# Gathers that skip the lanes without an edge, and a tile's first two slots added up later

## The chip, the cores and the metric

The kernel runs on one core of a Trainium2 chip. The metric is the device time of one execution in microseconds, the median of several runs. The core's engines each work through a queue of their own in order and wait for each other by semaphores: TensorE (PE in the profile; PEld are its weight loads), VectorE (DVE), ScalarE (ACT), GpSimd (POOL) and SyncE (SP). DMAs are issued by SyncE, ScalarE and GpSimd and run on 16 DMA engines. A gather, in which every partition fetches a row that an index in its memory names, is issued by GpSimd.

## What is computed

Two graph layers on 4096 nodes with 512 features. `adj` is a 4096 x 4096 matrix with about 8 nonzero weights a row beside the diagonal.

```python
# layer 0
a = adj + eye
d = sum(a, axis=1) ** -0.5
out = relu((d[:, None] * a * d[None, :]) @ x @ W.T + b)
x = layernorm(x + out)
# layer 1: attention whose scores are -1e16 wherever adj < 1 (off the diagonal too)
x = layernorm(x + attention(x, adj, Wks, Wqs, Wvs, Wo))
```

As the weights lie below 1, each row of layer 1 attends to itself alone, and the layer is a product with a fixed matrix. The kernel tests on the chip that this holds and has a general version behind a branch, which does not run with these inputs.

## The kernel before

The 4096 rows are 32 tiles of 128 rows. `few_edges_below_one` does the work in two halves.

**First half.** In a loop over tiles (L1064) the rows of `adj` are streamed in. ScalarE sums each row (`sum_rows`, L708) or the negative part of it (`sum_negative`), GpSimd makes the scaling d from it (`scaling`), and y = d * (x @ W.T) is computed tile by tile and stored to HBM (`keep_y`). SyncE loads the adjacency tiles: 13 of them pass through two buffers (`a_n`, pool `passing`), which ScalarE's sum frees; the others (`a_t`) have five. Along the way the weights of layer 1 are folded into one matrix `wvo` (`second_weights`): a generator hands out one step per turn of the loop, whose second part is run in the next turn (`left`, L1090). Its last step, `centre` (L650), subtracts column means on VectorE, which also gives row sums, and then shifts `wvo` by the row means in four activations on ScalarE.

**Finding the edges.** VectorE scans each tile of `adj` in eight segments of 512 columns. `MAX8` (L752) gives the eight largest values of a segment and `FIND_INDEX8` (L753) their columns. `sorting` packs segment, column and value bits into integer keys (`place` holds the segment's and the place's code), takes the 24 largest keys and unpacks from them column and weight. A key of 0 stands for no edge. `match` then hands the edges that a row has beyond nine to other lanes of the same tile that have room, by a permutation in a matmul, so that each tile ends with KH = 9 slots of 128 lanes: an index (`cols_all`), a weight and a target row each (`wr_all`). `match_end` (L890) writes them. A lane without an edge gets column 0 and weight 0. Scans, sorting and matching of the later tiles go on through most of the second half, spread over its steps (`some`).

**Second half.** The loop over tiles and slots (L1306, L1313) has 32 x 9 steps. In each step:

- `gather` (L1119, issued at L1124) makes GpSimd fetch the 128 rows of y for a slot that is AHEAD = 18 steps ahead, into one of 19 buffers `g`. A gather waits for its buffer's last reader.
- `build` makes ScalarE write the 128 x 128 matrix `s_t` for a slot (`spread`), which carries weights to target rows.
- TensorE multiplies it with the gathered rows and adds into the tile's sum `zs` in PSUM (L1337). In the trace each such product is two matmuls.
- `presum` (L1137): in tiles 1 to 22 the first two slots of a tile stay in their own rows. So they are added up beforehand: ScalarE scales slot 0 (L1141) at step 7 of the tile before, VectorE multiplies slot 1 by its weight and adds it (L1143) at step 8, and one product serves both, at step 0 of the tile. In the last nine tiles five slots are treated so.
- After a tile's last product, `scaled` and `residual` (VectorE), transposes and the product with `wvo` (TensorE, L703), variance and `finish` (ScalarE) make its output one to three tiles later.

The instructions are written in this order; the framework's scheduler sets the final order on each engine and the buffers, except where an instruction is marked to stay in place.

Of the kernel before, what the change touches and what calls it, by code (L numbers as in the profile page):

```python
# [11 lines left out]
ALU = mybir.AluOpType  # L12
# [407 lines left out]
def few_edges_below_one(  # L420
# [18 lines left out]
    nc = tc.nc  # L439
# [74 lines left out]
            ranks(sources[:, n + 1, lane + 1 - width : lane + 1], -2, 2 * r - 1 - P)  # L514

    place = const.tile([P, 2, C], U32, name="place")
    for f, (per_seg, per_edge, base, shift) in enumerate(
        ((-(C - 1), -SEGS, C * SEGS, 21), (-E, -1, C, 24))
    ):
        nc.gpsimd.iota(  # L520
            place[:, f], pattern=[[per_seg, SEGS], [per_edge, E]], base=base, channel_multiplier=0
        )
        nc.vector.tensor_scalar(place[:, f], place[:, f], shift, None, op0=ALU.logical_shift_left)


    v_all = const.tile([P, NT, C], FP, name="v_all")
# [31 lines left out]
    resident = list(range(last, NT))  # L558
    again = [t for t in range(last) if t not in early]
    order = early + resident + again  # L560
    def load_first(t, parts=1):
        if t in early or t in resident:
            return load_a(t, parts=2 if t == NT - 1 else parts)
        return load_a(t, pn, "a_n")
# [52 lines left out]
    def second_weights(su1):  # L617

        wo_sb, wvT = su1[:, 0], su1[:, 1]

        def transposed(r):
            pt = ps_t.tile([P, 512], FP, name="pt")
            for j in range(ND):
                nc.tensor.transpose(pt[:, ts(j, P)], w_nat[:, j, ts(r, P)], ident)
            return pt

        def put(r, pt):
            nc.scalar.copy(
                wvT[:, r, :].rearrange("q (p j) -> q j p", j=ND),
                pt[:, :D].rearrange("q (j p) -> q j p", j=ND),  # L630
            )

        def product(dc):
            pa = ps_a.tile([P, D], FP, name="acc")
            for r in range(NP):
                nc.tensor.matmul(
                    pa, wvT[:, r, ts(dc, P)], wo_sb[:, r, :], start=(r == 0), stop=(r == NP - 1)
                )
            return pa

        def add(dc, pa):
            nc.scalar.copy(wvo[:, dc, :], pa)
            nc.gpsimd.tensor_tensor(wvo[:, dc, ts(dc, P)], wvo[:, dc, ts(dc, P)], ident, ALU.add)

        def sums():
            pa = ps_a.tile([P, D], FP, name="acc")
            for dc in range(ND):
                nc.tensor.matmul(pa, ones, wvo[:, dc, :], start=(dc == 0), stop=(dc == ND - 1))
            return pa

        def centre(pa):
            row = const.tile([P, ND], FP, name="row")
            for dc in range(ND):
                nc.vector.scalar_tensor_tensor(
                    wvo[:, dc, :], pa, -1.0 / D, wvo[:, dc, :], op0=ALU.mult, op1=ALU.add,
                    accum_out=row[:, dc : dc + 1],
                )
            nc.vector.tensor_scalar(row, row, -1.0 / D, None, op0=ALU.mult)
            for dc in range(ND):
                nc.scalar.activation(  # L660
                    wvo[:, dc, :], wvo[:, dc, :], AF.Identity, bias=row[:, dc : dc + 1]
                )

        for r in range(NP):
            yield "t", (lambda r=r: transposed(r)), (lambda pt, r=r: put(r, pt))
        for dc in range(ND):
            yield "p", (lambda dc=dc: product(dc)), (lambda pa, dc=dc: add(dc, pa))
        yield "p", sums, centre

    def load_keys():  # L670
        su2 = setup_tile()
# [84 lines left out]
    def sorting(t, idx, rec):  # L756
# [16 lines left out]
        def stt(out, a, sc, b, op0, op1, **kw):  # L773
            return lambda: nc.vector.scalar_tensor_tensor(out, a, sc, b, op0=op0, op1=op1, **kw)  # L774
# [10 lines left out]
        def drop(f, r):  # L785
# [5 lines left out]

                stt(own, idx[:, home], spot[:, t % TS : t % TS + 1], v[:, home],
                    ALU.is_equal, ALU.mult, accum_out=own_all[:, t : t + 1]),
                stt(key[:, 0], idx, 12, place[:, 0], ALU.logical_shift_left, ALU.bitwise_or),
            ],
            [
                stt(key[:, 1], vu, 0x7FFFF, place[:, 1], ALU.bitwise_and, ALU.bitwise_or),
# [18 lines left out]
            [  # L816
                one(ints[:, 1], topu[:, 0], 0xFFF, 19, op0=ALU.bitwise_and,
                    op1=ALU.logical_shift_left),
                one(ints[:, 0], topu[:, 0], 12, 0xFFF, op0=ALU.logical_shift_right,
                    op1=ALU.bitwise_and),  # L820
            ],
            [
# [67 lines left out]
    def match_end(t, merged):  # L890
        wr = wr_all[:, t]
        nc.vector.tensor_copy(wr[:, 0:3], merged[:, 0:3])
        nc.vector.tensor_tensor(wr[:, 0:3], wr[:, 0:3], merged[:, 3:6], ALU.add)
        nc.vector.tensor_tensor(wr[:, 1], wr[:, 1], merged[:, 6], ALU.add)
        nc.vector.tensor_scalar(cols_all[:, t], wr[:, 0], float(N - 1), None, op0=ALU.min)
        if second:
            nc.scalar.activation(wr[:, 3], wr[:, 1], AF.Copy, scale=-1.0)
        else:
            nc.vector.tensor_scalar(wr[:, 3], wr[:, 1], -1.0, None, op0=ALU.mult)
# [160 lines left out]
        a_tiles[t] = load_first(t)  # L1060
    transpose_w()
    split_b()
    setup, left = iter(()), None
    for t in range(NT + 1):  # L1064
        if t == 0:
            su1 = load_second_weights()
        if t + DEEP < NT:
            a_tiles[t + DEEP] = load_first(t + DEEP)
        if t == 3:
            order_second_weights()  # L1070
            setup = second_weights(su1)

        ahead = sum(at <= projected(t) for at, _ in due)
        turn = sum(at <= projected(t + (t >= LEAD)) for at, _ in due)
        turn_rows(turn, 3)
        kind, begin, end = next(setup, (None,) * 3) if ahead - done[1] < 2 else (None,) * 3
        got = begin() if kind == "t" else None
        if t < NT:
            if t in early:
                sum_negative(t, a_tiles[t])  # L1080
            else:
                sum_rows(deg_all[:, t : t + 1], a_tiles[t][:, : N // 2 if t == NT - 1 else N])
                more = None
                if t == NT - 1:
                    more = small.tile([P, 1], FP, name="more")
                    sum_rows(more, a_tiles[t][:, N // 2 :])
                scaling(t, more)
            if t in again:
                del a_tiles[t]
        if left:  # L1090
            left()
            left = None
        for j in [j for at, j in due if at == t]:
            keep_y(j, us.pop(j))
        while done[1] < ahead:
            j = due[done[1]][1]
            us[j] = times(evacuate(p1, "xT", turned.pop(j), t >= NT - 7), wT)
            done[1] += 1
        turn_rows(turn, 2)
        if kind == "t":  # L1100
            end(got)
        if kind == "p":
            left = lambda end=end, pa=begin(): end(pa)
        if t < NT - 5:
            match(*ALL)
        some((t + 1) * RATE)
# [4 lines left out]

    mat = ctx.enter_context(tc.tile_pool(name="mats", bufs=3))
    p2 = ctx.enter_context(tc.tile_pool(name="second", bufs=2))
    AHEAD = 18

    summed = [1] + [2] * (NT - 1 - 9) + [SAME] * 9
    slots = {}

    def gather(j):  # L1119
        if j >= NT * KH:  # L1120
            return
        t, k = order[j // KH], j % KH
        slots[j] = p2.tile([P, D], FP, name="g", bufs=AHEAD + 1)
        nc.gpsimd.indirect_dma_start(  # L1124
            out=slots[j], out_offset=None, in_=y[:, :],
            in_offset=bass.IndirectOffsetOnAxis(ap=cols_all[:, t, k : k + 1], axis=0),
        )

    def load_own(i):
# [7 lines left out]
    def presum(i, k):  # L1137
        g = slots[i * KH]
        w = wr_all[:, order[i], 1, k : k + 1]
        if k == 0:  # L1140
            nc.scalar.activation(g, g, AF.Copy, scale=w)  # L1141
            return
        nc.vector.scalar_tensor_tensor(  # L1143
            g, slots.pop(i * KH + k), w, g, op0=ALU.mult, op1=ALU.add
        )

    def last_products(ks, c):

# [157 lines left out]
    for i in range(NT + 2):  # L1306
# [6 lines left out]
        for k in range(KH):  # L1313
# [7 lines left out]
            if i == NT - 1:  # L1321
# [8 lines left out]
                if k == 7:  # L1330
                    pts[i] = transpose_rows(hs[i], (0, 1))
                    hTs[i] = p2.tile([P, ND, P], FP, name="hT", bufs=2)
                    tc.keep_in_program_order(nc.scalar.copy(
                        hTs[i][:, 0:2].rearrange("p c s -> p (c s)"), pts[i][:, : 2 * P]
                    ))
            elif i < NT and not 0 < k < summed[i]:
                nc.tensor.matmul(  # L1337
                    zs[i], mats[i][:, KH if k < summed[i] > 1 else k, :], slots.pop(i * KH + k),
                    start=False, stop=(k == KH - 1),
                )  # L1340
            if i < NT:
                gather(i * KH + k + AHEAD)
            build(1)
            if i + 1 < NT and k >= KH - summed[i + 1] and summed[i + 1] > 1:
                presum(i + 1, k - (KH - summed[i + 1]))
            if k == 1 and has_p and not ends:
                scaled(p)
# [74 lines left out]
```

## Time and profile before

| | |
|---|---|
| median of 3 runs | 631.8 us (629.84 to 633.22) |
| profiled execution | 632.17 us, of it 630.3 us span |
| VectorE, TensorE, ScalarE, GpSimd busy | 555.0, 523.2, 497.7, 357.6 us |
| bytes moved | 217.68 MB, mean 345 GB/s |
| first gather begins, last ends | 220.8 us, 606.9 us |
| software queue (GpSimd's DMAs) | 28,192 packets, 92.30 MB |

The span is cut into 40 slices of 15.76 us in the page; a digit is the busy share of a slice in tenths.

```profile
PE   1599886699968052799897999999999999989793
DVE  5699999999999998799998999999999999854441
ACT  0859668688899858479978988998989899877751
POOL 5232323233323277677775667777777777777740
PEclk9999988999999566799998999999999999989898
DMA  8999999899999587999999999999999988888851
```

The first half ends in the fourteenth slice, where DMA and TensorE drop; from there on the gathers run. In a row of a group, the numbers behind the bar are the busy time in us and the mean of one in ns, and behind the next bar the idle time of the engine just before these instructions, with what ended most of it. In the timeline a row has its start, its duration, engine, line, operation and tiles, and in brackets the idle time before it and its releaser.

### The profile page before, as it was taken

The numbers are of one execution on the slowest core, as the hardware profiler recorded it, in microseconds if no ns is written. First come the engines' busy times: TensorE is split into PE (matmuls) and PEld (weight loads), VectorE is DVE, ScalarE is ACT, GpSimd is POOL, SyncE is SP. The second block draws the span as 40 slices with busy tenths as digits, with TensorE's granted clock in tenths as the row PEclk, the third lists the DMA queues.
The fourth block names the chain that finished last, engine by engine and source line by source line (L and its number), as shares of the span: only waits on it lengthen the run. The fifth ranks groups of instructions, "written<-read, shape, count | busy, mean of one in ns | idle before, by whom it ended". The sixth has DMA issues, their size and how long they took to land. (4 is left out here: it accounts for less than half of the span.)

```text
span 630.3 us, 7782 instructions
## 1 busy us (share of the span) xinstructions
PE 523.2 (83%) x1537; PEld 241.2 (38%) x1537; DVE 555.0 (88%) x2037; ACT 497.7 (79%) x1093; POOL 357.6 (57%) x465
## 2 busy tenths in 40 slices
PE   1599886699968052799897999999999999989793
PEld 1344333345423021344443444444444444433251
DVE  5699999999999998799998999999999999854441
ACT  0859668688899858479978988998989899877751
POOL 5232323233323277677775667777777777777740
PEclk9999988999999566799998999999999999989898
DMA  8999999899999587999999999999999988888851
GB/s 327 401 420 423 421 427 428 332 416 426 425 425 424 238 282 226 354 383 397 398 397 399 402 368 327 389 354 381 313 394 366 317 265 280 280 276 244 286 163 38
DMA packets 57273, 217.68 MB, mean 345 GB/s; under 512 B 8701, under 2 KB 9981, under 8 KB 52864
## 3 DMA queue, kind: packets, MB, share of 16 engines
q1 hardware_dynamic: 23888, 115.48, 46.1%
q0 software_dynamic: 28192, 92.30, 41.7%
q10 hardware_dynamic: 5136, 9.31, 4.0%
q14 instruction: 43, 0.35, 0.2%
q8 instruction: 14, 0.23, 0.1%
HBM read 200.28 MB, written 16.78 MB: 344 GB/s over the span
## 5 line engine op out<-in xcount | busy, mean ns | idle before, releaser
L1124 POOL DMA_INDIRECT g<-y,cols_all x288 | 286.9, 996 | 101.9 <-issue 46.6
L1337 PE MATMUL acc<-g,s_t 128*128 128x512 f32 x450 | 221.6, 626 | 38.4 <-DVE g L1143 22.2
L752 DVE MAX8 v_all<-a_t 128x8 f32<-128x512 f32 x256 | 166.7, 678 | 15.9 <-DMA a_t<-in_adj_dram 15.9
L753 DVE FIND_INDEX8 idx<-v_all,a_t 128x8 uint32<-128x512 f32 x256 | 173.2, 684 | 0.0
L703 PE MATMUL acc<-wT,xT 128*128 128x512 f32 x256 | 121.8, 625 | 20.6 <-ACT xT L694 19.8
L1337 PEld LDWEIGHTS acc<-g,s_t 128*128 128x128 f32 x450 | 84.2, 199 | 133.0 <-issue 101.0
L703 PE MATMUL acc<-wvo,hT 128*128 128x512 f32 x256 | 117.8, 602 | 5.2 <-ACT hT L694 4.2
L715 ACT ACTIVATE dump<-a_t 128x2048 uint8<-128x2048 f32 (+1 forms) x50 | 119.2, 2383 | 0.0
L703 PEld LDWEIGHTS acc<-wT,xT 128*128 128x128 f32 x256 | 49.2, 200 | 78.1 <-issue 53.1
L703 PEld LDWEIGHTS acc<-wvo,hT 128*128 128x128 f32 x256 | 48.8, 193 | 66.9 <-issue 57.0
L1006 ACT ACTIVATE sq<-cols,wr_all 128x128 f32<-128x128 f32 x160 | 58.8, 393 | 6.7 <-DMA a_t<-in_adj_dram 6.1
L1143 DVE SCALAR_TENSOR_TENSOR g<-g,wr_all 128x512 f32<-128x512 f32 x58 | 43.0, 741 | 23.4 <-ACT s_t L1016 6.6
L1010 ACT ACTIVATE s_t<-sq,wr_all 128x128 f32<-128x128 f32 x128 | 58.5, 485 | 0.2
L722 POOL TENSOR_SCALAR deg<-deg_all 128x1 f32<-128x1 f32 x32 | 7.3, 229 | 78.5 <-DVE deg_all L970 45.5
L710 ACT ACTIVATE dump<-a_n 128x4096 uint8<-128x4096 f32 x13 | 47.3, 3639 | 0.0
L550 POOL DMA_DIRECT2D x_t<-in_x_dram x32 | 18.0, 565 | 41.6 <-PE pt L689 35.4
L783 DVE MAX8 top<-key 128x8 f32<-128x64 f32 x192 | 36.2, 213 | 0.1
L1141 ACT ACTIVATE g<-g,wr_all 128x512 f32<-128x512 f32 x31 | 22.1, 713 | 16.4 <-issue 10.0
L694 ACT COPY hT<-pt 128x512 f32<-128x512 f32 x31 | 18.0, 579 | 18.1 <-PE pt L689 17.9
L774 DVE SCALAR_TENSOR_TENSOR key<-key,top 128x64 f32<-128x64 f32 x128 | 32.2, 272 | 0.0
L694 ACT COPY xT<-pt 128x512 f32<-128x512 f32 x32 | 18.9, 600 | 14.3 <-PE pt L689 12.4
L1194 DVE SCALAR_TENSOR_TENSOR h<-yo,own_all,acc 128x512 f32<-128x512 f32 (+1 forms) x33 | 23.7, 719 | 5.1 <-PE acc L1337 2.6
(135 smaller groups left out, 661.4 us busy)
## 6 DMA issues: line engine op xcount, KB each, us to landing
a_t<-in_adj_dram SPq DMA_DIRECT2D x17, 2048.0 KB, 21.5
a_t<-in_adj_dram SPq DMA_DIRECT2D x56, 512.0 KB, 12.4
a_n<-in_adj_dram SPq DMA_DIRECT2D x13, 2048.0 KB, 15.8
x_t<-in_x_dram POOLq DMA_DIRECT2D x32, 256.0 KB, 11.3
yo<-y SPq DMA_DIRECT2D x32, 256.0 KB, 6.5
x_t<-in_x_dram SPq DMA_DIRECT2D x32, 256.0 KB, 7.3
out_dram<-r_t ACTq DMA_DIRECT2D x31, 256.0 KB, 6.1
y<-y_t POOLq DMA_DIRECT2D x18, 256.0 KB, 14.7
```

The costliest lines, as they stand in the source:

```text
L694: copy = nc.scalar.copy(dst.rearrange("p c s -> p (c s)"), pt[:, :D])
L703: nc.tensor.matmul(u, srcT[:, dc, :], w[:, dc, :], start=(dc == 0), stop=(dc == ND - 1))
L710: nc.scalar.activation(dump[:, : part.shape[1]], part, AF.Copy, accum_out=dst)
L715: nc.scalar.activation(dump[:, o], a_t[:, o], AF.Relu, scale=-1.0, accum_out=neg_all[:, t, halves[0] : halves[0] + 1],)
L752: long.append(lambda o=o, seg=seg: nc.vector.max(v[:, o], seg))
L753: long.append(lambda o=o, seg=seg: nc.vector.max_index(idx[:, o], v[:, o], seg))
L783: return lambda: nc.vector.max(top[:, f, r * 8 : r * 8 + 8], keyf[:, f])
L1006: nc.scalar.activation(sq, cols1, AF.Square, bias=wr[:, 2, k : k + 1])
L1010: nc.scalar.activation(s_t[:, k, :], away(), AF.Relu, scale=wr[:, 3, k : k + 1], bias=wr[:, 1, k : k + 1],)
L1124: nc.gpsimd.indirect_dma_start(out=slots[j], out_offset=None, in_=y[:, :], in_offset=bass.IndirectOffsetOnAxis(ap=cols_all[:, t, k : k + 1 ...
L1143: nc.vector.scalar_tensor_tensor(g, slots.pop(i * KH + k), w, g, op0=ALU.mult, op1=ALU.add)
L1337: nc.tensor.matmul(zs[i], mats[i][:, KH if k < summed[i] > 1 else k, :], slots.pop(i * KH + k), start=False, stop=(k == KH - 1),)
```

## The change

**Indices.** The keys are built so that a lane without an edge comes out as index 8191 instead of 0, beyond the 4096 rows, and the real ones as 8191 minus a number of 4096 and more. `place` is made of other numbers, an `or` in the key becomes an `xor`, the mask of the index has 13 bits for 12, and `match_end` turns the number around in place of a minimum with N - 1. `gather` is given a bound, N - 1, and told that an index beyond it is no error: such a row is skipped, and its lane keeps what the buffer held. In the first three tiles, whose gathers fill the 19 buffers for the first time, an operation more forces a valid index (`unskipped`).

**First two slots.** In tiles 1 to 22 the scaling comes at step 8 of the tile before, the multiply-add at step 1 of the tile, their product at step BASE = 3. Slots 2, 3 and 4 are multiplied at steps 0, 1 and 2, slots 5 to 8 at steps 4 to 7, and step 8 has no product.

**Shift of `wvo`.** The four activations at the end of `centre` become a step of their own, `shift`, run a turn of the first half's loop later.

```diff
@@ few_edges_below_one: codes of the keys
-        ((-(C - 1), -SEGS, C * SEGS, 21), (-E, -1, C, 24))
-    ):
+    per_code = 2 * SEGS
+        (per_code * E - 1, per_code, per_code - 1, N.bit_length() - 1 + 12 - (SEGS.bit_length() - 1), (SW - 1) << 12),
+        (E, 1, 1, 24, 0),
+    )):
...
-        nc.vector.tensor_scalar(place[:, f], place[:, f], shift, None, op0=ALU.logical_shift_left)
+        nc.vector.tensor_scalar(
+            place[:, f], place[:, f], shift, fill,
+            op0=ALU.logical_shift_left, op1=ALU.bitwise_or,
+        )
@@
+    AHEAD = 18
+    ABSENT = 2 * N - 1
+    unskipped = order[: -(-(AHEAD + 1) // KH)]
@@ second_weights: centre
             nc.vector.tensor_scalar(row, row, -1.0 / D, None, op0=ALU.mult)
+            return row
+
+        def shift(row):
             for dc in range(ND):
-                nc.scalar.activation(
+                tc.keep_in_program_order(nc.scalar.activation(
                     wvo[:, dc, :], wvo[:, dc, :], AF.Identity, bias=row[:, dc : dc + 1]
-                )
+                ))
...
         yield "p", sums, centre
+        yield "s", None, shift
@@ sorting
-                stt(key[:, 0], idx, 12, place[:, 0], ALU.logical_shift_left, ALU.bitwise_or),
+                stt(key[:, 0], idx, 12, place[:, 0], ALU.logical_shift_left, ALU.bitwise_xor),
...
-                one(ints[:, 0], topu[:, 0], 12, 0xFFF, op0=ALU.logical_shift_right,
+                one(ints[:, 0], topu[:, 0], 12, ABSENT, op0=ALU.logical_shift_right,
@@ match_end
-        nc.vector.tensor_scalar(cols_all[:, t], wr[:, 0], float(N - 1), None, op0=ALU.min)
+        if t in unskipped:
+            nc.vector.tensor_scalar(
+                wr[:, 0], wr[:, 0], float(ABSENT - (N - 1)), None, op0=ALU.max
+            )
+        nc.vector.tensor_scalar(
+            cols_all[:, t], wr[:, 0], -1.0, float(ABSENT), op0=ALU.mult, op1=ALU.add
+        )
@@ loop of the first half
-        if left:
-            left()
-            left = None
+        row = (left() if left else None) or row
+        left = None
...
+        if kind == "s":
+            left = lambda end=end, row=row: end(row)
@@ gather
             in_offset=bass.IndirectOffsetOnAxis(ap=cols_all[:, t, k : k + 1], axis=0),
+            bounds_check=N - 1, oob_is_err=False,
@@ loop of the second half
+    BASE = 3
...
+    def product(i, m, j, stop):
+
+        nc.tensor.matmul(zs[i], mats[i][:, m, :], slots.pop(j), start=False, stop=stop)
...
+            elif i < NT and summed[i] == 2:
+                if k == BASE:
+                    product(i, KH, i * KH, False)
+                else:
+                    m = k + 2 if k < BASE else k + 1
+                    if m < KH:
+                        product(i, m, i * KH + m, m == KH - 1)
             elif i < NT and not 0 < k < summed[i]:
-                nc.tensor.matmul(
-                    zs[i], mats[i][:, KH if k < summed[i] > 1 else k, :], slots.pop(i * KH + k),
-                    start=False, stop=(k == KH - 1),
-                )
+                product(i, KH if k < summed[i] > 1 else k, i * KH + k, k == KH - 1)
...
-            if i + 1 < NT and k >= KH - summed[i + 1] and summed[i + 1] > 1:
+            if i + 1 < NT and summed[i + 1] == 2 and k == KH - 1:
+                presum(i + 1, 0)
+            if i < NT and summed[i] == 2 and k == 1:
+                presum(i, 1)
+            if i + 1 < NT and k >= KH - summed[i + 1] and summed[i + 1] > 2:
                 presum(i + 1, k - (KH - summed[i + 1]))
```

More of the change, by code (lines that the diff above doesn't have):

```diff
@@ L516, in few_edges_below_one @@
     place = const.tile([P, 2, C], U32, name="place")
-    for f, (per_seg, per_edge, base, shift) in enumerate(
-        ((-(C - 1), -SEGS, C * SEGS, 21), (-E, -1, C, 24))
-    ):
+    per_code = 2 * SEGS
+    for f, (per_seg, per_edge, base, shift, fill) in enumerate((
+        (per_code * E - 1, per_code, per_code - 1, N.bit_length() - 1 + 12 - (SEGS.bit_length() - 1), (SW - 1) << 12),
+        (E, 1, 1, 24, 0),
+    )):
         nc.gpsimd.iota(
@@ L1062, in few_edges_below_one @@
     split_b()
-    setup, left = iter(()), None
+    setup, left, row = iter(()), None, None
     for t in range(NT + 1):
@@ L1113, in few_edges_below_one @@
     p2 = ctx.enter_context(tc.tile_pool(name="second", bufs=2))
-    AHEAD = 18
+    BASE = 3
     summed = [1] + [2] * (NT - 1 - 9) + [SAME] * 9
```

## The prediction

> **What bounds the kernel.** I read the page first (busy shares, then the forty slices), then the groups, then GpSimd's own timeline and sums over stretches. The page's busy shares mislead here:
>
> ```profile
> PE 523.2 (83%) x1537; PEld 241.2 (38%) x1537; DVE 555.0 (88%) x2037; ACT 497.7 (79%) x1093; POOL 357.6 (57%) x465
> L1124 POOL DMA_INDIRECT g<-y,cols_all x288 | 286.9, 996 | 101.9 <-issue 46.6
> L550 POOL DMA_DIRECT2D x_t<-in_x_dram x32 | 18.0, 565 | 41.6 <-PE pt L689 35.4
> L722 POOL TENSOR_SCALAR deg<-deg_all 128x1 f32<-128x1 f32 x32 | 7.3, 229 | 78.5 <-DVE deg_all L970 45.5
> ```
>
> GpSimd looks like the idlest engine at 57%. But 286.9 us of it lie in one line, the 288 gathers of the second half, and 101.9 us of idle time sit directly before them, put down mostly to "issue", a wait for nothing that the profile shows. The timeline of GpSimd explains this:
>
> ```profile
> 333.83 0.94 POOL L1124 DMA_INDIRECT g<-y,cols_all  x1 [0.30 <-DMA g<-y,cols_all]
> 336.53 0.94 POOL L1124 DMA_INDIRECT g<-y,cols_all  x1 [1.75 <-PE acc L1337]
> 337.77 0.95 POOL L1124 DMA_INDIRECT g<-y,cols_all  x1 [0.30 <-DVE rec L780]
> 339.02 0.95 POOL L1124 DMA_INDIRECT g<-y,cols_all  x1 [0.30 <-issue]
> 342.51 1.09 POOL L1124 DMA_INDIRECT g<-y,cols_all  x1 [2.54 <-DVE key L774]
> ```
>
> Whatever is named as releaser, the smallest gap is 0.30 us. So a gather costs 0.95 + 0.30 = 1.25 us of GpSimd (206 of the 287 steps from one gather to the next are below 1.26 us). The first begins at 220.8 and the last ends at 606.9, 386.2 us, of which 288 x 1.25 = 360 us is this price, 14.5 us are gathers longer than 0.946 us (63 of them), and 11.9 us (summed over the timeline) are gaps beyond 0.30, like the 1.75 and 2.54 above. **The second half is a queue of gathers**; everything else fits beside it or just does not:
>
> ```profile
> 440.00:518.00 78.00, 78.00 (x236) 35.35 (x235) 77.95 (x322) 72.42 (x213) 59.28 (x60) 1.00 0.94 334
> ```
>
> In this stretch (its columns: length, PE, PEld, DVE, ACT, POOL busy, clock, DMA) 60 gathers x 0.30 + 59.28 = 77.3 of 78 us: GpSimd is full, and so is TensorE, which takes 11.54 us for a tile of nine gathers where GpSimd takes 11.25 us and some 0.4 of lengthening. Two engines are tied. TensorE falls behind only where it idles:
>
> ```profile
> 236.99 0.32 PE L855 MATMUL pt<-ident,rank_key 128*128 128x128 f32 x1
> 248.27 10.18 PE L1337 MATMUL acc<-g,s_t 128*128 128x512 f32 x16 [10.96 <-DVE g L1143]
> 263.13 1.22 PE L1337 MATMUL acc<-g,s_t 128*128 128x512 f32 x1 [4.14 <-DVE g L1143]
> ```
>
> These are the waits for the presum, the multiply-add of a tile's first two slots on VectorE: 22.2 us in 8 waits. Each leaves the ring of 19 buffers full later, and GpSimd then waits for "PE acc L1337": the 11.9 us.
>
> **The change, part by part.**
>
> *Presum later.* For tiles 1 to 22 the scaling moves one step, the multiply-add two steps, and their product three steps later; the products of slots 2, 3 and 4 come before it. Nothing is added: same instructions, same queues, 32 x 9 gathers. The product of a slot takes two matmuls, 2 x 0.43 = 0.86 us, so 2.6 us of work now stand ahead of the wait. From the 10.96 and the 4.14 us waits that takes 2.6 each; the waits of 1.62, 0.59, 0.94 and 1.29 us at 314, 327, 342 and 369 go whole (VectorE has 4 steps where it had 2). Sum 9.6 us. The two late waits (1.02 and 1.67 us, after 545) are of tiles with five summed slots, which don't change. What is late next is GpSimd, so this is not 9.6 us of its own: it is the larger part of the 11.9 us of GpSimd's excess gaps, and counts once. Slots 2 to 4 are needed two steps (2.5 us) earlier, 16 steps or 20 us after their issue; they land in 6.7 us (longest 11.2). Slot 0's buffer is held three steps longer, slot 2's to 8's less; when the buffers come free in order, the lead falls from 18 to 16 steps, at most 2 x 1.25 = 2.5 us once.
>
> *The shift of wvo, moved to the next turn of the first half.* ScalarE stood there for VectorE's row sums:
>
> ```profile
> 116.59 2.56 ACT L660 ACTIVATE wvo<-wvo,row 128x512 f32<-128x512 f32 x4 [4.01 <-DVE row L658]
> GB/s 327 401 420 423 421 427 428 332 416 426 425 425 424 238 282 226 354 383 397 398 397 399 402 368 327 389 354 381 313 394 366 317 265 280 280 276 244 286 163 38
> ```
>
> The eighth slice (110 to 126 us) moves 332 GB/s where its neighbours move 428 and 416: (422 - 332) x 15.76 us / 422 = 3.4 us of lost transfer in a stage that DMA fills to the end, since the next adjacency load waits for the buffer that the late row sum on ScalarE frees. The 4.01 us wait goes, the four activations stay. I take -3 us; ends 0 (other gaps follow) and -4.
>
> *Keys and indices.* Same number of VectorE instructions for a tile; one more in the first three tiles, 3 x 0.19 us by L895's mean for the same shape, hidden in VectorE's queue, which is busy half the time or less from 551 on: nothing.
>
> *The bound.* This is the unknown, and it is multiplied by 288. What it saves: 9 lanes for 8.03 edges a row leave 3,959 lanes empty in these inputs, 460 of them in the three tiles that are not skipped, so 3,499 of 36,864 rows, 13.4 for each of 261 gathers, 7.2 MB of 217.7. DMA transfers were not what the gathers waited for (TensorE waited 0.7 us for one), so the bytes are worth nothing here. What it costs on GpSimd, no row shows. Nearest rows: a plain DMA of 128 rows is 0.565 us, the gather 0.946, so indices cost 0.38 us, 3.0 ns each. Lower end: the test is free and a skipped index saves its 3 ns: -0.04 us. Upper end by rows: one GpSimd operation over 128 single values, dispatch included, L722, +0.229 us. A rule speaks against the change: the Trainium skill, GPSIMD Engine Reference, section 3.1, states that data-dependent branching costs about 12 cycles an element, at 1.2 GHz 10 ns. As estimates from that page, a branch that only skipped rows pay is 0.134 us x 261 = 35 us; one that all 128 indices pay is 1.28 us a gather, 369 us. By the rows the sum is -12 to +66 us. I can't rule the rule out, since nothing in this trace branches on data; the second reading I take as too dear, as a gather handles an index in 3 ns. I take the middle of the rows' ends, **+0.09 us a gather**, near the rule's first reading: 288 x 0.09 = +26 us.
>
> **Sum.** Span 630.3. If GpSimd is dearer than 1.25 us it no longer meets a full ring, TensorE's 11.54 us a tile lie under 9 x 1.34 + 0.4 = 12.5 us, and all 11.9 us of excess gaps vanish, whichever way: 630.3 - 11.9 - 3 + 26 = 641.4. Around the span lie 632.17 - 630.3 = 1.9 us; the profiled execution is 0.4 above the median of 631.8. So **643**, and in general 616.9 + 288 x price.
>
> **The rivals.** A difference below 0.5%, 3.2 us, can't be told from none.
> (A, forecast) The bound makes the gather dearer by 0.06 to 0.22 us: 634 to 680. For it: GpSimd has 0.7 us of 78 to spare; the rule. Against it: no row of a bounded gather.
> (B, not slower) The test is free or pays for itself. Then TensorE's 11.54 us a tile bound tiles 3 to 22 again, so a cheaper gather brings little beyond the waits: 632 - 3 - 9.6 = 619, with 0.04 us cheaper gathers gaining some 3 us in the last nine tiles, whose TensorE work is 8.9 us: 616 to 628. The point from which it loses is a price of 15 / 288 = 0.05 us.
> (C) The price lies at that point and eats the gain: 629 to 635.
> (D) The bound doesn't spare the descriptors (the skipped rows are fetched, or each row gets a packet of its own in a stage whose DMA share is 1.0 from 264 to 400): as A or B for time, but with software-queue bytes unchanged at 92.3 MB. With rows packed singly, DMA could replace GpSimd as the bound; the trace gives no price, and I leave it to A's upper end.
>
> **How the numbers follow.** A 0.57, its own range 634 to 680; B 0.32; C 0.11. The two signs hold most of the chance, so the range spans both: 616 to 674, which leaves out a gather dearer by over 0.2 us and a gain beyond B's. Faster 0.32, same 0.11, slower 0.57.
>
> **What would show it.** The group of L1124: mean 996 ns and its smallest durations; by the forecast about 1.04 us typical in place of 0.946, and cadence 1.34; B has 0.95 or less. Longer gathers where more lanes are empty (the last slots of a tile) would mean that skipping is the cost, an equal rise in all that the test is. Software-queue bytes should fall by 7 MB. TensorE's waits for L1143 should fall from 22 to about 12 us, its waits for gathers rise (A). ScalarE's 4 us wait at 113 should go and the first gather start near 218. The forecast is wrong if the gather's typical duration is below 1.0 us, or if the second half lengthens while the gathers stand at 1.25.

## The result, and the profile after

| | before | after |
|---|---|---|
| median of 22 runs each, side by side | 630.85 us (626.50 to 634.16) | 634.99 us (631.66 to 638.27) |
| ratio after / before | | 1.0056, 95% interval 1.0039 to 1.0073 |
| profiled execution, its span | 632.17, 630.3 us | 632.32, 630.4 us |
| typical gather (median), gap after it | 0.946, 0.305 us | 0.998, 0.305 us |
| first gather begins, last ends | 220.8, 606.9 us | 221.4, 608.9 us |
| GpSimd's gaps beyond 0.305 us between gathers | 11.9 us | 0.8 us |

The kernel became slower by 0.56%, 3.5 us (2.5 to 4.6 by the interval); the medians lie 4.1 us apart. The forecast was 643 us, 11 us above before. The profiled execution of after is among its quickest and that of before is above its median, so the two spans agree by chance. The price of a gather does not depend on that; gaps, lengthened gathers and the tail may.

The group of the gathers, the software queue and the busy shares, from the page of after (the gather is now at L1143):

```profile
PE 528.4 (84%) x1537; PEld 240.6 (38%) x1537; DVE 556.0 (88%) x2040; ACT 496.4 (79%) x1093; POOL 369.5 (59%) x465
q0 software_dynamic: 28192, 85.15, 38.9%
L1143 POOL DMA_INDIRECT g<-y,cols_all x288 | 299.3, 1039 | 90.8 <-issue 40.6
```

GpSimd is busy 12 us longer, all of it in this line, and the idle time in front of its gathers is 11 us shorter. The mean of 1039 ns mixes typical with lengthened gathers. The view of a single line gives minimum, median and maximum in ns, here of before and then of after:

```profile
L1124 POOL DMA_INDIRECT g<-y,cols_all x288: 940/946/1822, 220.8 to 606.0; - x144
```

```profile
L1143 POOLq MOVE  x288: 29/29/29, 218.3 to 600.4; - x144
L1143 POOL DMA_INDIRECT g<-y,cols_all x288: 992/998/1913, 221.4 to 607.9; - x144
```

Minimum and median rose by the same 52 ns. Sorted by the nine slots of a tile, every slot's median is 0.998 or 0.999; the 27 gathers of the first three tiles, which skip nothing, show the same. The bound also put a register move of 29 ns before each gather, on the engine's sequencer. So the price is one per gather, 288 x 0.052 = 15.0 us, and not one per row. GpSimd's timeline, in the same stretch that was shown of before:

```profile
333.83 1.00 POOL L1143 DMA_INDIRECT g<-y,cols_all  x1 [0.31 <-issue]
335.14 0.99 POOL L1143 DMA_INDIRECT g<-y,cols_all  x1 [0.30 <-issue]
336.44 1.00 POOL L1143 DMA_INDIRECT g<-y,cols_all  x1 [0.30 <-DMA g<-y,cols_all]
337.74 1.00 POOL L1143 DMA_INDIRECT g<-y,cols_all  x1 [0.30 <-PE acc L1169]
339.04 1.06 POOL L1143 DMA_INDIRECT g<-y,cols_all  x1 [0.31 <-DVE rec L843]
```

A step is 1.30 us, and the gaps of 1.75 and 2.54 us are gone. GpSimd's waits for TensorE's release of a buffer, summed between 218 and 610 us (total in us, times, longest), before and then after:

```profile
POOL g L1124 <- PE acc L1337: 20.1, 47, 2.6
```

```profile
POOL g L1143 <- PE acc L1169: 13.4, 43, 0.5
```

The number of times hardly changed, because the name of a releaser is put even on a bare 0.30 us gap. The last column is the one to read: the longest fell from 2.6 to 0.5 us. GpSimd no longer meets a full ring.

**The ledger** from the first gather's start to the last one's end: +15.0 (price), -11.1 (gaps), -2.6 (gathers longer than the median: 14.5 us of it before, 11.9 after), in sum +1.3; the first one starts 0.6 later: +1.9, where the last end moved by 2.0. The tail after it is 1.9 us shorter. So the ledger accounts for this pair of executions, which differ by 0.2 us, and not for the 4 us between the medians.

TensorE's waits for the presum, from its timeline (the product of the sum is now the fourth of a tile):

```profile
239.81 1.10 PE L1169 MATMUL acc<-g,s_t 128*128 128x512 f32 x2 [2.03 <-DMA g<-y,cols_all]
248.95 6.31 PE L1169 MATMUL acc<-g,s_t 128*128 128x512 f32 x10 [5.57 <-DVE g L1163]
258.34 1.10 PE L1169 MATMUL acc<-g,s_t 128*128 128x512 f32 x2 [1.81 <-DMA g<-y,cols_all]
```

The wait of 10.96 us fell to 5.57, but the product itself starts at 248.95 where it started at 248.27: it waits less because TensorE reaches it later. New in front of it are waits for gathers, of slots that are now needed sooner. The later waits for the presum did not go. In before, then in after:

```profile
314.34 2.84 PE L1337 MATMUL acc<-g,s_t 128*128 128x512 f32 x6 [1.62 <-DVE g L1143]
327.17 2.84 PE L1337 MATMUL acc<-g,s_t 128*128 128x512 f32 x6 [0.59 <-DVE g L1143]
342.30 4.54 PE L1337 MATMUL acc<-g,s_t 128*128 128x512 f32 x6 [0.94 <-DVE g L1143]
```

```profile
312.44 1.12 PE L1169 MATMUL acc<-g,s_t 128*128 128x512 f32 x2 [1.80 <-DVE g L1163]
327.28 1.12 PE L1169 MATMUL acc<-g,s_t 128*128 128x512 f32 x2 [1.29 <-DVE g L1163]
341.18 2.03 PE L1169 MATMUL acc<-g,s_t 128*128 128x512 f32 x2 [2.05 <-DVE g L1163]
```

With one more, at 369 us in before and at 391 us in after, these waits come to 4.4 us in before and to 5.8 us in after.

The shift of `wvo`, in ScalarE's timeline of after:

```profile
121.49 2.57 ACT L671 ACTIVATE wvo<-wvo,row 128x512 f32<-128x512 f32 x4
138.24 0.69 ACT L748 ACTIVATE y_t<-acc,d_all 128x512 f32<-128x512 f32 x1 [4.39 <-POOL d_all L737]
141.70 0.58 ACT L706 COPY xT<-pt 128x512 f32<-128x512 f32 x1 [2.78 <-PE acc L715]
```

It waits for nothing now. But from 134 us on ScalarE stands for 4.39 and then 2.78 us, and the slices show the hole at another place:

```profile
GB/s 326 400 423 423 423 424 427 424 424 384 419 426 425 184 267 215 379 381 388 396 395 388 357 349 321 347 346 357 287 340 357 275 249 244 255 243 230 256 168 39
```

The eighth slice has 424 instead of 332, the tenth 384 instead of 426, the fourteenth 184 instead of 238.

### The profile page after: what moved, and what is told of

The parts are those of the page before. It is cut to its first block, busy times and chain, and to the rows that moved or that the text cites. A ratio compares the mean times of both kernels' runs of the same rounds, so it can differ in the third digit from the quotient of the medians.

```text
span 630.4 us, 8099 instructions
## 1 busy us (share of the span) xinstructions
PE 528.4 (84%) x1537; PEld 240.6 (38%) x1537; DVE 556.0 (88%) x2040; ACT 496.4 (79%) x1093; POOL 369.5 (59%) x465
## 2 busy tenths in 40 slices
DMA packets 57276, 210.55 MB, mean 334 GB/s; under 512 B 10260, under 2 KB 11540, under 8 KB 52864
## 3 DMA queue, kind: packets, MB, share of 16 engines
q0 software_dynamic: 28192, 85.15, 38.9%
HBM read 200.28 MB, written 16.78 MB: 344 GB/s over the span
## 5 line engine op out<-in xcount | busy, mean ns | idle before, releaser
L1143 POOL DMA_INDIRECT g<-y,cols_all x288 | 299.3, 1039 | 90.8 <-issue 40.6
L1169 PE MATMUL acc<-g,s_t 128*128 128x512 f32 x450 | 224.1, 624 | 36.1 <-DVE g L1163 16.5
L715 PE MATMUL acc<-wT,xT 128*128 128x512 f32 x256 | 125.7, 642 | 15.2 <-ACT xT L706 15.1
L1169 PEld LDWEIGHTS acc<-g,s_t 128*128 128x128 f32 x450 | 81.2, 196 | 131.7 <-issue 72.4
L715 PEld LDWEIGHTS acc<-wT,xT 128*128 128x128 f32 x256 | 50.8, 207 | 75.3 <-issue 56.2
```

The lines of the kernel that those rows point to most:

```text
L715: nc.tensor.matmul(u, srcT[:, dc, :], w[:, dc, :], start=(dc == 0), stop=(dc == ND - 1))
L1143: nc.gpsimd.indirect_dma_start(out=slots[j], out_offset=None, in_=y[:, :], in_offset=bass.IndirectOffsetOnAxis(ap=cols_all[:, t, k : k + 1 ...
L1169: nc.tensor.matmul(zs[i], mats[i][:, m, :], slots.pop(j), start=False, stop=stop)
```

## The experiments

**Theory**: the second half is GpSimd's queue of gathers; the bound's test is a flat price on each gather, part of which the ring's gaps swallow. **Rivals**: the price lies with the rows that are skipped; TensorE bounds as much as GpSimd, so that its waits and not the gathers set the time.

Times are medians, and microseconds that go with a ratio are worked out from the ratio. Waits and gaps are read from one profiled execution of each kernel, and executions of one kernel differ by several us (before: 626.50 to 634.16), so a difference of 3 us in gaps or waits is a hint and no more.

**The bound alone, on the kernel before.** Indices, presum and shift stay old, so no index lies beyond the bound and nothing is skipped.

```diff
             in_offset=bass.IndirectOffsetOnAxis(ap=cols_all[:, t, k : k + 1], axis=0),
+            bounds_check=N - 1, oob_is_err=False,
```

> The kernel before with the bound given to each gather and nothing else; every index is valid, so no row is skipped. Theory (the test has a flat price that GpSimd pays for each gather): gather 0.998 us as in the changed kernel, 288 x 0.052 = +15 us of gathers, of which the 11.9 us of ring waits swallow most: 633 to 637, ratio 1.004 to 1.009. Rival 1 (the later presum is what kept the changed kernel near the time before): the ring waits stay and the time rises by the whole 15 us, ratio about 1.024. Rival 2 (skipping, not testing, is dear): gather 0.946 us, ratio 1.000.

Measured: 638.48 us beside 630.8, ratio 1.0138 (1.0101 to 1.0176). The line's view:

```profile
L1124 POOLq MOVE  x288: 29/29/29, 217.7 to 606.8; - x144
L1124 POOL DMA_INDIRECT g<-y,cols_all x288: 992/998/2181, 220.8 to 613.2; - x144
```

The 52 ns are there without a skipped row. (`bounds_check` and `oob_is_err` were only ever given together, so the price is that of both.) The ratio falls between the two expectations: the price is 15.0 us, the gaps went from 11.9 to 3.9 and so swallowed 8.0. 15.0 - 8.0 = 7 us, where the ratio gives 8.7 and the medians 7.7. The theory's "all gaps vanish" was too strong for the old presum.

**The presum alone.** The diff's part for the first two slots, nothing else.

```diff
+            elif i < NT and summed[i] == 2:
+                if k == BASE:
+                    product(i, KH, i * KH, False)
...
+            if i + 1 < NT and summed[i + 1] == 2 and k == KH - 1:
+                presum(i + 1, 0)
+            if i < NT and summed[i] == 2 and k == 1:
+                presum(i, 1)
```

> The kernel before with the presum moved later and nothing else. Theory: gather 0.946 us; TensorE's waits for the presum fall from 22 us to about 13, GpSimd's gaps beyond 0.30 us fall from 11.9 to 2 to 7 us, and the time falls by 4 to 9 us: ratio 0.985 to 0.994. Rival (TensorE is tied with GpSimd by its own 11.54 us a tile, so that the waits come back elsewhere): gaps stay near 11 us, ratio 0.997 to 1.003.

Measured: 628.46 us, ratio 0.9976 (0.9954 to 0.9998), a quarter of what the theory said. VectorE's timeline of this kernel, then of before, shows a part of the reason (L1144 here and L1143 there is the multiply-add of tile 1):

```profile
246.80 0.75 DVE L1199 SCALAR_TENSOR_TENSOR h<-yo,own_all,acc 128x512 f32<-128x512 f32 x1
247.58 0.69 DVE L1207 SCALAR_TENSOR_TENSOR h<-h,x_t 128x512 f32<-128x512 f32 x1
248.20 0.75 DVE L1144 SCALAR_TENSOR_TENSOR g<-g,wr_all 128x512 f32<-128x512 f32 x1
```

```profile
247.47 0.75 DVE L1143 SCALAR_TENSOR_TENSOR g<-g,wr_all 128x512 f32<-128x512 f32 x1
```

VectorE works through a backlog in order, and the multiply-add now stands behind one operation more: it starts 0.7 us later, of the 2.6 us by which its reader moved. TensorE's waits for it fell from 22.2 to 19.1 us only, GpSimd's excess gaps from 11.9 to 8.7.

**The shift alone.** `centre` returns `row`, and the four activations run a turn later, as in the diff.

```diff
+            return row
+
+        def shift(row):
...
         yield "p", sums, centre
+        yield "s", None, shift
```

> The kernel before with the four activations that shift wvo moved one turn later and nothing else. Theory (a stall of ScalarE for GpSimd and TensorE, 4.4 and 2.8 us in the changed kernel, takes the place of the 4.0 us one): the first gather begins at 220 to 222 us as before, ratio 0.998 to 1.002. Rival (the prediction's 3 us are there and the changed kernel lost them by a throttled clock): first gather at 217 to 218 us, ratio 0.994 to 0.996.

Measured: 630.92 us, ratio 1.0003 (0.9979 to 1.0027): nothing, as the theory's time said, though the first gather came at 226.45, later than either expected. In this execution the last gather ended at 606.2 all the same (before: 606.9): gaps of 8.3 us in place of 11.9 and shorter gathers made up for a start 5.7 us later. So the start of the gathers is not handed on to the end one to one. ScalarE's largest waits of the first half in this kernel (total, times, longest):

```profile
ACT xT L698 <- PE acc L707: 11.0, 3, 7.8
ACT y_t L740 <- POOL d_all L729: 3.8, 2, 3.3
```

The stall of 4.0 us for the row sums is replaced by others. The wait for GpSimd's scaling stands at 137.98, as in after.

**Presum and shift together.**

> The kernel before with presum and shift moved, without the bound and with the old indices. Theory: the sum of the two runs before it, 4 to 9 us faster than before, ratio 0.985 to 0.994, gather 0.946 us. Rival (neither is worth anything while GpSimd and TensorE are tied): ratio 0.997 to 1.003.

Measured: 628.95 us, ratio 0.9968 (0.9950 to 0.9987). The two parts do not add up to more than the presum alone; excess gaps 7.9 us.

**The change without skipping.** All 32 tiles get valid indices; the bound stays.

```diff
-    unskipped = order[: -(-(AHEAD + 1) // KH)]
+    unskipped = order
```

> The changed kernel with all 32 tiles forced to valid indices, so that the bound is tested and no row is skipped. Theory (a flat price of the test, bytes worth nothing): gather 0.998 us, software queue 92.3 MB, ratio to before 1.003 to 1.010, like the changed kernel's 1.0056. Rival (skipped rows pay back part of the price through 7 MB less of transfers): ratio 1.010 to 1.016.

Measured: 636.28 us, ratio 1.0094 (1.0059 to 1.0129), median gather 0.998, software queue at 92.30 MB again. The interval overlaps that of the change (1.0056). The 7.2 MB less are worth little or nothing; the two ratios lie 2.4 us apart, and a gain of up to some 5 us can't be excluded.

**The change without the bound.** Valid indices everywhere, and the argument taken out.

```diff
-            bounds_check=N - 1, oob_is_err=False,
```

> The changed kernel with the bound taken out and all indices forced valid; keys, presum and shift stay as changed. Theory (the bound alone makes the change slower): gather 0.946 us, ratio to before 0.993 to 0.999, some 6 us below the changed kernel. Rival (the reversed order of a row's edges or the keys have a part in it): ratio above 1.002.

Measured: 628.57 us, ratio 0.9959 (0.9940 to 0.9978). The line's view:

```profile
L1143 POOL DMA_INDIRECT g<-y,cols_all x288: 940/946/2107, 221.6 to 601.2; - x144
```

The gather is back at 0.946. The bound is all that makes the change slower, and without it the rest of the change gains 2.6 us, not the 12.6 of the prediction's case B.

**Bound and skipping, on the old presum and shift.** Of the diff only keys, indices and the bound.

> The kernel before with keys, bound and skipped rows of the changed one, presum and shift as before. Theory (skipping is worth nothing in time): gather 0.998 us, ratio 1.010 to 1.018, as with the bound alone. Rival (skipping pays back): ratio 1.003 to 1.009.

Measured: 637.98 us, ratio 1.0121 (1.0074 to 1.0167), beside 1.0138 with nothing skipped; median gather 0.998, software queue 85.15 MB. Again skipping shows no worth outside the intervals. From here to after the median falls by 3 us, by presum and shift: with the dearer gather they let the gaps go (4.8 us here, 0.8 in after).

**Every row skipped.** In all tiles but the first three each index lies beyond the bound, so 261 gathers fetch no row and the sums lack these rows.

```diff
         nc.vector.tensor_scalar(
-            cols_all[:, t], wr[:, 0], -1.0, float(ABSENT), op0=ALU.mult, op1=ALU.add
+            cols_all[:, t], wr[:, 0], -1.0 if t in unskipped else 0.0, float(ABSENT),
+            op0=ALU.mult, op1=ALU.add,
         )
```

> The changed kernel with every index of tiles outside the first three set beyond the bound, so that 261 gathers fetch no row at all (the output then lacks these rows). Theory (the price is the test's, per gather): 0.998 us for these 261 as for the 27 that fetch all rows. Rival 1 (a skipped row saves its 3 ns): 0.6 to 0.7 us. Rival 2 (a skipped row pays a branch of 10 ns): 1.6 us or more.

Measured in one execution: 631.0 us. The line's view, and lines of the page:

```profile
L1144 POOL DMA_INDIRECT g<-y,cols_all x288: 992/998/1862, 221.4 to 608.3; - x144
```

```profile
q0 software_dynamic: 28192, 24.02, 12.0%
DMA packets 57276, 149.42 MB, mean 238 GB/s; under 512 B 25405, under 2 KB 26685, under 8 KB 52864
```

61 MB less than in after, and the gather takes 0.998 us all the same, whether it fetches 128 rows or none. This refutes both readings of the branching rule that the prediction weighed, 0.134 us where rows are skipped and 1.28 us for all indices: the cost has no part that goes with the rows skipped. A gather's time on GpSimd does not depend on its bytes either. For the time of the kernel that is not shown: the one execution is quicker than the quickest of after's 22 (631.66), so 61 MB less may be worth some us.

**Only the product later.** Product of the sum at step 3, the multiply-add at its old place in VectorE's queue.

```diff
+            elif i < NT and summed[i] == 2:
+                if k == BASE:
+                    product(i, KH, i * KH, False)
...
             if i + 1 < NT and k >= KH - summed[i + 1] and summed[i + 1] > 1:
                 presum(i + 1, k - (KH - summed[i + 1]))
```

> The kernel before with only the product of the presum moved to step 3 (slots 2 to 4 multiplied first); scaling and multiply-add stay at steps 7 and 8 of the tile before, no bound. Theory (in the later presum VectorE's multiply-add moved two steps down a queue that is itself behind, so TensorE gained one step, not three): here the slack is three steps; TensorE's waits for the multiply-add fall from 20.5 us (after 220 us) to under 12, against 16 with the presum moved too, and the ratio to before is 0.988 to 0.995, below the 0.9976 of that run. Rival (the waits are not what bounds; GpSimd and TensorE take turns): the waits fall but the ratio stays at 0.995 to 1.000.

Measured: 628.30 us, ratio 0.9969 (0.9952 to 0.9985). The waits for the presum are 16.4 us, not below 12 as expected. The interval overlaps that of the whole move (0.9976): it does not tell the two placings apart. The four waits between 300 and 400 us are 1.00, 1.11, 1.61 and 0.44 us here, 4.2 in sum beside 4.4 in before, though the multiply-add kept its place.

**The product last.** As the one before, with the product of the sum after the tile's other seven.

```diff
-    BASE = 3
+    BASE = KH - 2
...
+                if k == BASE:
+                    product(i, KH, i * KH, True)
+                elif k < BASE:
+                    product(i, k + 2, i * KH + k + 2, False)
```

> As the run before it, with the product of the presum as the last of its tile (step 7, slots 2 to 8 first). Theory: the waits for the multiply-add in tiles 1 to 22 are gone but for the first one, GpSimd's gaps beyond 0.30 us fall below 4 us, ratio 0.984 to 0.992. Rival (as above): ratio 0.995 to 1.000, with waits for gathers or for ScalarE in their place.

Measured: 627.01 us, ratio 0.9934 (0.9911 to 0.9956), 4.2 us faster than before and the lowest of the versions that leave nothing out, though its interval overlaps those of others. TensorE's waits in it:

```profile
PE acc L1150 <- DVE g L1144: 7.7, 6, 4.1
PE acc L1150 <- DMA g<-y,cols_all: 7.5, 9, 3.2
```

14.5 us of waits for the presum went, 6.8 us of waits for gathers came. GpSimd's excess gaps stayed at 8.2 us where under 4 were expected. So, as far as one execution of each can tell, the presum's waits are not, as the prediction had it, the source of all of the 11.9. The summed stretch shown of before, in this kernel:

```profile
440.00:518.00 78.00, 74.72 (x226) 33.72 (x224) 77.97 (x317) 71.70 (x212) 59.18 (x61) 1.00 0.93 331
```

TensorE has 3 us to spare here, and VectorE, the third of the busy times, has none: 77.97 of 78 us.

**Eight gathers a tile.** Slot 8 uses the rows of slot 7; its own rows are left out, and 256 gathers remain.

```diff
         t, k = order[j // KH], j % KH
+        if k == KH - 1:
+            slots[j] = slots[j - 1]
+            return
```

> The kernel before with 8 of a tile's 9 gathers: slot 8 is multiplied with the rows of slot 7 (so the last slot's rows are left out of the sum), everything else stays. Theory (GpSimd and TensorE are tied in the tiles before the last nine; GpSimd alone bounds the last nine): TensorE's 11.54 us a tile stay, the last nine tiles fall toward 9 us each: 12 to 25 us faster, ratio 0.960 to 0.981. Rival 1 (GpSimd alone bounds the half): 32 x 1.25 = 40 us faster, ratio about 0.937. Rival 2 (TensorE alone bounds): ratio above 0.99.

Measured: 620.46 us, ratio 0.9849 (0.9809 to 0.9888). 32 gathers less are 40 us less for GpSimd, and 10 us of them arrive at the end. The summed stretch shown of before, in this kernel:

```profile
440.00:518.00 78.00, 78.00 (x240) 35.36 (x239) 77.94 (x322) 72.43 (x215) 53.62 (x55) 1.00 0.89 311
```

TensorE has no gap left and still takes 11.54 us for a tile; GpSimd has gaps of 36 us in all. Most of what was gained came from the last nine tiles, in which five slots are summed and TensorE needs less: 78.4 us from the first product of tile 23 to that of tile 31, where before took 87.9. Close behind GpSimd there is a next bound, and it need not be TensorE: VectorE is as full in this row, 77.94 of 78 us, and so it was in before (77.95). The prediction, which called TensorE and GpSimd tied, left VectorE out.

**Eight products a tile.** Slot 8's product left out, all gathers kept.

```diff
-            elif i < NT and not 0 < k < summed[i]:
+            elif i < NT and k < KH - 1 and not 0 < k < summed[i]:
```

> The kernel before with all 9 gathers and without the product of slot 8 in all tiles but the last (its rows are left out of the sum): TensorE's tile falls by 0.86 us. Theory (tied): GpSimd's price stays, only its ring waits go: 4 to 11 us faster, ratio 0.983 to 0.994. Rival 1 (GpSimd alone bounds): ratio above 0.997. Rival 2 (TensorE alone bounds): 31 x 0.86 = 27 us faster, ratio about 0.957.

Measured: 762.43 us, ratio 1.212 (1.206 to 1.218). This miss says nothing of the question: from 303 to 682 us a gather waited 3 to 10 us once in every tile. A buffer that nobody reads seems to have been held until much later; that is inferred from the waits, not tested.

**A short last product.** Slot 8 is multiplied for 128 of its 512 columns, the rest of that product is left out, and slot 7's product follows it, at step 8; every buffer keeps its reader.

```diff
+                    nc.tensor.matmul(
+                        zs[i][:, :P], mats[i][:, k, :], slots.pop(i * KH + k)[:, :P],
+                        start=False, stop=False,
+                    )
```

> In place of the run with eight products, whose unread buffers held up the ring: the kernel before with all 9 gathers, and slot 8 multiplied for 128 of the 512 columns only (the other columns of its rows are left out of the sum), in all tiles but the last. TensorE's tile falls by about 0.6 us, to 10.9. Theory (tied; GpSimd's price stays and only its ring waits go): 3 to 10 us faster, ratio 0.984 to 0.995. Rival 1 (GpSimd alone bounds): ratio above 0.997. Rival 2 (TensorE alone bounds): 31 x 0.6 = 19 us faster, ratio about 0.970.

The first time it ran where TensorE's granted clock fell to half, mostly for 7 us, after every 24 us or so at full; before took 700.39 us there, and 1.0191 (1.0023 to 1.0360) is not comparable with the rest. It was run again:

> The same kernel as in the run before it, which fell on a chip that halved TensorE's clock every 24 us or so (the kernel before took 700 us there). Theory (tied): GpSimd's price stays, its ring waits go: ratio 0.984 to 0.995. Rival 1 (GpSimd alone bounds): above 0.997. Rival 2 (TensorE alone bounds): about 0.970.

Measured: 631.18 us beside 630.44, ratio 1.0007 (0.9990 to 1.0023). The stretch, and TensorE's longest waits:

```profile
440.00:518.00 78.00, 76.17 (x243) 34.72 (x241) 77.84 (x316) 70.72 (x210) 58.47 (x59) 1.00 0.94 335
```

```profile
PE acc L1345 <- DVE g L1143: 33.3, 16, 12.2
```

TensorE needs 10.93 us for a tile instead of 11.54 (495.80 to 506.73 us, where it does not wait), and the time did not move: 11 us of what it saved became waits for the presum (33.3 us instead of 22.2), and GpSimd's excess gaps are 11.4, as before. Tiles 12 to 22 came every 11.36 us instead of 11.57, with VectorE busy for 77.84 of 78 us. With the eight gathers this gives the order of the two "tied" engines: a faster TensorE alone brings nothing, and a faster GpSimd alone brings some 10 us, until TensorE or VectorE stops it. Which of these two comes first is open, since no run gave VectorE less to do: with eight gathers the even 11.54 us of tiles 12 to 22 speak for TensorE, and here a freed TensorE soon waits for VectorE.

## Why the prediction was off

**Right: the bound of the second half and the sign.** In after GpSimd issues from the first gather to the last with 0.8 us of gaps, its price counts 288 times, and a dearer gather makes the kernel slower although fewer bytes move. In before it holds less well: the row from which the prediction read "two engines are tied" shows three, since VectorE is busy for 77.95 of the same 78 us. The prediction's mark "an equal rise in all that the test is" is what came. Its formula, 616.9 + 288 x price, gives 631.9 at the measured price and 634.9 without the 3 us for the shift; 634.99 was measured. That closeness owes something to luck: the profiled execution of before lies above its median, and the shorter gathers and the shorter tail (2.6 and 1.9 us in the traces) stand in no term. The marks for the bytes (-7 MB) and for the rising waits on gathers (0.7 to over 5 us) came too.

**The step that failed: "+0.09 us a gather".** It was the middle between -0.04 and +0.229 us, two rows that are both about something else, with a rule about data-dependent branches beside it. Measured: 0.052 us, 15.0 us in place of 26. This term alone was 11 us too large; with the measured 15.0 for the price, -11.1 for the gaps and 0 for the shift the sum is +3.9 us, where the ratio gives 3.5 and the medians 4.1. The -0.04 end rested on a skipped index saving its share of the duration: no row saves anything. The +0.229 end was a whole GpSimd operation; the test adds no operation of its own, only a register move. The point from which it loses was put at 0.05, so the result lies just beyond it, and the time lies in case C, which was given 0.11, as much as in A. By its own mark ("typical duration below 1.0 us") the forecast was wrong, by 2 ns.

**The shift, "I take -3".** It measured 0 (1.0003), and in after the first gather starts 0.6 us later instead of 3 earlier. The bandwidth lost in a slice was real, but SyncE's loads wait for the buffers that ScalarE frees (73.1 us of it between 100 and 215 us in before, 70.5 in after), and once ScalarE's stall for the row sums went, a stall of 4.4 us for GpSimd's scaling came 20 us later. The 0 was one of the step's two ends. ScalarE's queue should have been followed through the next turns. The second half of the step, that an earlier first gather means an earlier end, is not borne out either by the run of the shift alone.

**The presum, "sum 9.6 us".** TensorE's waits fell by 5.7 us in after and 3.1 alone, against 9.6; and in time the move together with the shift is worth 2.6 us (2.0 in the run on the kernel before with the old indices), not the 12.6 that case B gave to both. The first two waits fell by 8.1 us in after, more than the 5.2 forecast; the four that were to "go whole" rose from 4.4 to 5.8. "VectorE has 4 steps where it had 2" would hold for an idle VectorE. It is busy for 250.0 of the 254 us from 264 to 518 in before and 250.5 in after, and gives the multiply-add when its queue gets there, so that TensorE spends at one presum what it saved before it. That the multiply-add moved along is the smaller part: with it in its old place the four waits were still 4.2 us. This cause is read from busy times and waits; no run with a lighter VectorE tests it.

**"All 11.9 us of excess gaps vanish, whichever way".** In after 11.1 did; with the bound on the old presum 8.0; with the presum alone 3.2. They vanish nearly whole where both come together, which was this case. Here the sum was right, and its reason half right: product last, which took two thirds of the presum's waits away, left 8.2 us. Where these come from stays open; VectorE, busy for 97% and more of the time from 264 to 518 us in before, in after and here, is the first suspect.

Open too: whether skipping by itself gains a little. Both pairs of runs that differ in it alone lean that way (1.0056 and 1.0094; 1.0121 and 1.0138), within their intervals.

## What to carry to other kernels

Where the bound is an engine that issues one small operation after another, whatever is added to the operation counts as often as it runs: measure that price on one line before weighing the bytes that it saves, since bytes that nobody waits for are worth little or nothing. A wait for an engine that is busy all the time is hardly shortened by moving its reader: look first how full the writer's queue is, for every engine of the row and not only for the two that seem tied. And a stall that goes in a stage of coupled queues is worth its length only after the queue has been followed to the next wait.

## What the runs showed of the hardware

- The bound of an indirect DMA costs the same 52 ns for 0, 13 or 128 rows skipped out of 128, with a register move of 29 ns on the sequencer beside it.
- Skipped rows leave small packets behind. The count is 57,276 in after and with all rows of 261 gathers skipped (57,273 in before), but packets under 512 B rose from 10,260 in after to 25,405 with all rows skipped. In before it was 8,701, and the difference from there is 16,704 = 261 x 64: a gather of 128 rows makes 64 packets of two rows, and an emptied packet stays. The packet sizes in the trace of after agree: 1,559 packets of 8 bytes and 381 of 2,052 bytes, 2 x 1,559 + 381 = 3,499 skipped rows, the number that the prediction counted. A skipped row leaves 4 bytes.
- The page's count of bytes read from HBM did not follow: 200.28 MB before, in after, and with 68 MB of the gathers left out. In this kernel it is no measure of what the gathers fetched.
